# 3x3 convolution products as two 128x64 array tiles with two runs of 64 positions

## The chip, the cores and the metric

The kernel runs on one core of a Trainium2 chip. The metric is the device time of one execution in microseconds, as the median of several runs. A TensorE product of two float32 operands shows in the profile as two passes, each with one weight load (LDWEIGHTS, on the row called PEld) and one matrix multiplication (MATMUL, on the row called PE). In this text a *pass* is one such pair of records.

## What is computed

The input x has 8 images of 512 channels and 32x32 positions. After a group normalisation the layer computes, in float32:

```python
t = cbs(x, cv1_w, cv1_bn, 0)            # 1x1 convolution, batch norm, SiLU
ys = [t[:, :C], t[:, C:]]               # C = 256 channels each
for i in range(N):                      # N = 2
    yi = ys[-1]
    z = cbs(yi, m_cv1_w[i], m_cv1_bn[i], 1)              # the 3x3 convolution, 256 -> 256
    z = bot_attention(z, m_qkv_w[i], m_rw[i], m_rh[i])   # 4 heads of 64 over 1024 positions
    z = silu(bn_eval(conv2d(z, m_cv2_w[i], 0), m_cv2_bn[i]))
    ys.append(yi + z)
return cbs(concatenate(ys, axis=1), cv2_w, cv2_bn, 0)    # and x is added
```

The change concerns the line with the 3x3 convolution. It runs twice for each image, 16 times in all.

## The kernel before, in words

**Images and stages.** A Python loop runs over the 8 images, so the program is a straight list of instructions. For each image and each of the two bottlenecks the stages follow each other: `tiles_in` (VectorE transforms the input of the 3x3 convolution), `conv3x3`, the projection to queries, keys and values (`project_strassen`, lines L630 and L634, in image 0 a plain one), attention in a fast form (`attention_fast`), `m2` (L994). Between them lie the first 1x1 convolution of the next image (L386 or L1140) and the last one of this image (L1028). A scheduler orders the instructions of each engine when the program is built, by priorities and by the `issue_after` marks in the source; each engine then runs its own list in that order, with semaphores between engines.

**The 3x3 convolution.** It is done by a Winograd scheme: input and weights are transformed so that the convolution becomes sums of plain products, and the results are transformed back. `tiles_in` writes three tiles `vs[i]` (i = 0, 1, 2, called `v_in` in the profile), each with 2 channel blocks `k`, 2 rows, 4 columns and 128 positions. The weights `us[i]` have the same three pairs, made by `make_u` in image 0 (`u_new`) and loaded from DRAM afterwards (`u`), with 128 output channels for each block. For each half `oc` of the 256 output channels and each pair i, `conv3x3` takes a PSUM tile of 128 partitions x 2 rows x 4 columns x 128 positions[...]. It fills each of the eight blocks with a sum of two products over k (L970). A product has the whole 128x128 weight block as the stationary operand and 128 positions as the moving one. `columns_out` then reads the PSUM tile (ScalarE at L452, VectorE at L453 to L456), and `rows_out` (L473 to L481) finishes the transform.

**Other products that matter here.** In attention, the logits (L734) and the products with v (L768) use 64x64 tiles of the array, four of them side by side, over 512 positions. The row sums of attention (L786) use four tiles of 128 rows by 32 columns over 256 positions. All products of L386, L630, L634, L994, L1028 and L1140 use the whole 128x128 array.

**Order.** All products are in one queue of TensorE. SyncE issues loads, GpSimd issues stores and some loads; VectorE and ScalarE transform, evict PSUM and compute the exponentials. [...]

Of the kernel before, what the change touches and what calls it, by code (L numbers as in the profile page):

```python
# [56 lines left out]
HD = 64  # L57
# [4 lines left out]
def kernel(  # L62
# [16 lines left out]
    nc = tc.nc  # L79
# [5 lines left out]
    NM = C // P  # L85
# [233 lines left out]
    SLOT = (0, 1, 3, 2)  # L319
# [44 lines left out]
    def stages(act, small, ps_big, ps_av, n_pt):  # L364


        def silu(dst, src, k):

            return nc.scalar.activation(dst, src, AF.Silu, scale=sh[:, k : k + 1], bias=bh[:, k : k + 1])  # L369
# [3 lines left out]
        def table_of(func):  # L373

            return nc.scalar.activation(spare, zero, func)
# [73 lines left out]
        def columns_out(r, ps):  # L449

            m2 = act.tile([P, 2, NT * NW], F32, tag="h", name="m2", bufs=2)
            nc.scalar.copy(m2, ps[:, :, 2, :])  # L452
            nc.vector.tensor_tensor(r[..., 0], ps[:, :, 1, :], m2, ALU.add)  # L453
            nc.vector.tensor_tensor(r[..., 1], ps[:, :, 1, :], m2, ALU.subtract)
            nc.vector.scalar_tensor_tensor(r[..., 0], ps[:, :, 0, :], 2.0, r[..., 0], ALU.mult, ALU.add)
            nc.vector.scalar_tensor_tensor(r[..., 1], ps[:, :, 3, :], -2.0, r[..., 1], ALU.mult, ALU.add)  # L456

        def rows_out(dst, r12, r34, ends):


            sd = act.tile([P, 2, 2, NT * F], F32, tag="acc", name="sd", bufs=2)
            s_, d_, big_s, big_d = sd[:, 0, 0], sd[:, 0, 1], sd[:, 1, 0], sd[:, 1, 1]
            stt, tt = nc.vector.scalar_tensor_tensor, nc.vector.tensor_tensor

            def tiles(ap):
                return ap.rearrange("p (t w) -> p t w", w=F)

            def to(r):
                return dst.rearrange("p (t r w) -> p r t w", r=4, w=F)[:, r]

            def first():
                for i, rr in enumerate((r12, r34)):
                    tt(sd[:, i, 0], rr[:, 0], rr[:, 1], ALU.add)  # L473
                    tt(sd[:, i, 1], rr[:, 0], rr[:, 1], ALU.subtract)
                stt(to(1), tiles(big_d), -0.5, tiles(d_), ALU.mult, ALU.add)
                return tt(to(2), tiles(s_), tiles(big_s), ALU.subtract)

            def last():
                stt(ends, ends, -6.0, sd[:, 0], ALU.mult, ALU.add)
                stt(to(0), tiles(big_s), -0.25, tiles(ends[:, 0]), ALU.mult, ALU.add)  # L480
                stt(to(3), tiles(big_d), -2.0, tiles(ends[:, 1]), ALU.mult, ALU.add)  # L481

            return first, last
# [121 lines left out]
        def first_sum(z):  # L605

            t = act.tile([P, 4, HALF], F32, tag="pt", name="t_z", bufs=n_pt)
            nc.vector.tensor_tensor(t[:, 0], z[:, 0, ts(1, HALF)], z[:, 0, ts(0, HALF)], ALU.subtract)
            return t
# [345 lines left out]
        def conv3x3(n, vs, u_of, summed=False):  # L955
            t = None
            z = act.tile([P, NM, HW], F32, tag="z", name="z")
            for oc in range(NM):
                us = u_of(oc)
                r = act.tile([P, 2, 2, NT * NW, 2], F32, tag="acc", name="r_mid", bufs=2)  # L960
                ends = act.tile([P, 2, NT * NW, 2], F32, tag="rs", name="r_ends", bufs=2)
                rs = (r[:, 0], r[:, 1], ends)
                flat = [a.rearrange("p r q o -> p r (q o)") for a in rs]
                first, last = rows_out(z[:, oc, :], *flat)
                for i in range(PAIRS):
                    ps = ps_big.tile([P, 2, NC, NT * NW], F32, tag="big", name="c3_ps")
                    for row in range(2):
                        for col in range(NC):
                            for k in range(NM):
                                nc.tensor.matmul(  # L970
                                    ps[:, row, col, :], us[i][:, k, row, SLOT[col], :], vs[i][:, k, row, col, :],
                                    start=(k == 0), stop=(k == NM - 1),
                                )
                    columns_out(rs[i], ps)
                    if i == 1:
                        mid = first()
                        if oc == NM - 1 and summed:
                            with tc.issue_after(mid.ins):
                                t = first_sum(z)
                last()  # L980
                for half in range(NH):
                    part = z[:, oc, ts(half, HALF)]
                    last_silu = silu(part, part, bn_m1[n] + oc)
            with tc.issue_after(last_silu.ins):
                table_of(AF.Exp)
            return z, t
# [270 lines left out]
    us = {}  # L1257
# [63 lines left out]
    with tc.issue_after(made.ins):  # L1321
        vs = s.tiles_in(ypad[0])
    load_bottleneck(0)
    nxt = None
    for b in range(B):
# [6 lines left out]
        def u_of(n):  # L1332
            def of(oc):
                nonlocal last_load
                if b == 0 and n == 0 and oc == 1:
                    with tc.issue_after(last.ins):
                        for i in range(PAIRS):
                            make(n, oc, [i])
                got = [us.pop((oc, i)) if (oc, i) in us else load_u(n, oc, i) for i in range(PAIRS)]
                if (b > 0 or n > 0) and oc == 1:  # L1340
                    sq[n], last_load = load_sq(n)
                return got

            return of
# [40 lines left out]
        def first():  # L1385
            nonlocal nxt, six
            if more:
                nxt = new_y0()
            if more and b > 0:
                six = s.strassen_cv1(w1, sw, xs, nxt, y1n)  # L1390
                six[0]()
            elif more:
                s.cv1(w1, xs, nxt, y1n, Y1S[: NM // 2])
            else:
                parts[1] = s.cv2_part(w1, (y0, y1), 1)
# [34 lines left out]
        vs = s.tiles_in(y2)  # L1430
# [56 lines left out]
        if more:  # L1487
            three[2](y2, ylast, last, stored)
            with tc.issue_after(last.ins):
                vs = s.tiles_in(y1n)  # L1490
# [97 lines left out]
```

## Time and profile before

| | before |
|---|---|
| time, median of 3 runs | 2313.61 us (2312.37 to 2314.16) |
| span of the profiled execution, first to last instruction | 2311.5 us |
| the median run less this span | 2.1 us |
| TensorE multiplications, busy | 2286.2 us (99%) |
| TensorE weight loads, busy | 1172.4 us (51%) |
| VectorE, busy | 1840.2 us (80%) |
| ScalarE, busy | 987.6 us (43%) |
| granted TensorE clock, mean | 0.998 |
| products of the 3x3 convolutions (L970), busy | 306.1 us for 2720 passes and 41.5 us for 352 |

The profile comes from one execution. Its time is known as the span from the first to the last instruction; the device time of a run holds a little more around it. A busy time counts every moment in which an engine has at least one instruction under way, so overlapping matmuls are counted once, while the mean duration of one is longer than the distance from one to the next. A line number such as L970 is the line of the statement in the kernel's source.

### The profile page before, as it was taken

What the parts mean: (1) busy time and instruction counts of PE and PEld (TensorE: products, weight loads), DVE (VectorE), ACT (ScalarE), POOL (GpSimd) and SP (SyncE); (2) the same over time, 40 slices, a digit from 0 to 9 for tenths busy, and PEclk for the clock granted to TensorE, in tenths of its full rate; (3) what the DMA queues carried; (4) which work ended last, traced back from release to release, by engine and by line L of the source; (5) the groups of instructions that cost most, each with busy time, mean ns of one, the idle gap of its engine ahead of it and who ended that gap; (6) DMA issues with size and microseconds to landing.
All of it is one profiled execution on the core that took longest, in us unless ns stands there. A gap on an engine that the chain in (4) does not pass through costs nothing.

```text
span 2311.5 us, 36527 instructions
## 1 busy us (share of the span) xinstructions
PE 2286.2 (99%) x14806; PEld 1172.4 (51%) x14806; DVE 1840.2 (80%) x2920; ACT 987.6 (43%) x1292; POOL 89.1 (4%) x308
## 2 busy tenths in 40 slices
PE   7999999999999999999999999999999999999998
PEld 4546355463554636446364553646436364473643
DVE  8888878888788877887788887788877988777774
ACT  2443524435154452544525354253542525335352
POOL 1000000000000000000000000000000000000000
PEclk9999999999999999999999999999999999999999
DMA  7422333041430415213161221603116030260201
GB/s 239 174 86 87 120 134 154 16 151 34 174 118 26 136 48 202 76 53 108 52 240 37 76 87 47 250 29 102 59 47 250 29 133 29 75 221 16 87 11 62
DMA packets 95521, 235.60 MB, mean 102 GB/s; under 512 B 28016, under 2 KB 50736, under 8 KB 81904
## 3 DMA queue, kind: packets, MB, share of 16 engines
q1 hardware_dynamic: 83600, 182.84, 23.3%
q0 software_dynamic: 11744, 50.34, 5.7%
q8 instruction: 119, 1.95, 0.3%
q14 instruction: 58, 0.48, 0.1%
HBM read 198.54 MB, written 34.60 MB: 101 GB/s over the span
## 4 chain that ended last, share of the span: by engine, by line
PE 96%; DVE 3%; ACT 0%; DMA 0%; POOL 0%; issue 0%; SPq 0%; DVEq 0%; ACTq 0%
PE av_ps L768 19%; PE l_ps L734 19%; PE c_ps L970 14%; PE c L1028 8%; PE p_ps L630 8%; PE x_ps L1140 6%; PE c_new L1028 6%; PE m_ps L994 5%; PE ps L386 4%; PE pv_ps L634 3%; PE s_ps L786 1%; PE p_ps L634 1%; PE s_ps L804 1%; DVE acc L754 0%; PE v_ps L595 0%; DMA x<-in_x_dram 0%
## 5 line engine op out<-in xcount | busy, mean ns | idle before, releaser
L738 ACT ACTIVATE pt<-l_ps 128x1024 f32<-128x1024 f32 x512 | 494.8, 1023 | 410.1 <-PE l_ps L734 385.5
L754 DVE TENSOR_TENSOR acc<-acc,pt 128x1024 f32<-128x1024 f32 x384 | 469.5, 1223 | 65.5 <-ACT pt L738 40.0
L768 PE MATMUL av_ps<-pt,vT 64*64 64x512 f32 x4096 | 486.4, 591 | 0.5 <-DVE ao L776 0.5
L734 PE MATMUL l_ps<-q,kr 64*64 64x512 f32 x4096 | 485.9, 590 | 0.0
L970 PEld LDWEIGHTS c_ps<-v_in,u 128*128 128x128 f32 x2720 | 306.0, 192 | 6.7 <-issue 6.7
L970 PE MATMUL c_ps<-v_in,u 128*128 128x128 f32 x2720 | 306.1, 275 | 0.0
L768 PEld LDWEIGHTS av_ps<-pt,vT 64*64 64x64 f32 x4096 | 159.2, 133 | 269.4 <-issue 225.1
L734 PEld LDWEIGHTS l_ps<-q,kr 64*64 64x64 f32 x4096 | 160.0, 133 | 263.3 <-issue 252.2
L452 ACT COPY m<-c_ps 128x256 f32<-128x256 f32 x96 | 35.4, 369 | 216.3 <-PE c_ps L970 213.6
L1028 PE MATMUL c_new<-t_in,ws 128*128 128x512 f32 x288 | 124.6, 592 | 0.0
L994 PE MATMUL m_ps<-ao,m_sb 128*128 128x512 f32 x256 | 112.5, 592 | 0.0
L369 ACT ACTIVATE m_kept<-m_kept,bh,sh 128x512 f32<-128x512 f32 x42 | 31.9, 805 | 146.0 <-DVE m_kept L1112 86.3
L752 DVE TENSOR_TENSOR acc<-pt 128x1024 f32<-128x1024 f32 x64 | 78.1, 1220 | 18.0 <-ACT pt L738 18.0
L1028 PEld LDWEIGHTS c_new<-t_in,ws 128*128 128x128 f32 x288 | 54.7, 190 | 68.9 <-issue 66.0
L630 PE MATMUL p_ps<-t_z,sq 128*128 128x512 f32 x180 | 87.1, 593 | 0.0
L369 ACT ACTIVATE t<-m_ps,bh,sh 128x512 f32<-128x512 f32 x64 | 48.1, 776 | 83.9 <-PE m_ps L994 82.5
L994 PEld LDWEIGHTS m_ps<-ao,m_sb 128*128 128x128 f32 x256 | 48.6, 190 | 61.2 <-issue 61.0
L369 ACT ACTIVATE z<-z,bh,sh 128x512 f32<-128x512 f32 x64 | 48.6, 806 | 56.1 <-DVE z L481 56.1
L1002 DVE TENSOR_TENSOR ylast<-t,ypad 128x512 f32<-128x512 f32 x32 | 22.0, 692 | 63.2 <-ACT t L369 63.2
L445 DVE TENSOR_TENSOR v_in<-w_rows 128x512 f32<-128x512 f32 x96 | 65.6, 683 | 0.0
L453 DVE TENSOR_TENSOR r_mid<-c_ps,m 128x256 f32<-128x256 f32 x64 | 27.1, 423 | 46.5 <-ACT m L452 46.5
L1028 PE MATMUL c<-ypad,ws 128*128 128x512 f32 x144 | 63.8, 592 | 0.0
(255 smaller groups left out, 2997.3 us busy)
## 6 DMA issues: line engine op xcount, KB each, us to landing
u<-u SPq DMA_DIRECT2D x85, 1024.0 KB
x<-in_x_dram SPq DMA_DIRECT2D x32, 512.0 KB
x_res<-in_x_dram POOLq DMA_DIRECT2D x32, 512.0 KB, 6.9
out_dram<-m_kept POOLq DMA_DIRECT2D x28, 512.0 KB, 7.3
u<-u_new POOLq DMA_DIRECT2D x12, 1024.0 KB, 6.3
w<-in_cv_w_dram SPq DMA_DIRECT2D x12, 1024.0 KB
rs<-r_dram SPq DMA_DIRECT2D x96, 128.0 KB
ws<-s SPq DMA_DIRECT2D x24, 512.0 KB
```

The costliest lines, as they stand in the source:

```text
L369: return nc.scalar.activation(dst, src, AF.Silu, scale=sh[:, k : k + 1], bias=bh[:, k : k + 1])
L386: last_product[0] = nc.tensor.matmul(ps[:, half, :], w_of(k), rhs_of(k, half), start=(k == begin), stop=(k == end))
L630: nc.tensor.matmul(ps[:, o, :], w[:, o, :], rhs, start=not onto, stop=True, skip_group_check=onto)
L634: nc.tensor.matmul(v[:, ts(j, P)], rhs[:, ts(j, P)], w[:, 2, :], start=j == 0 and not onto, stop=True, skip_group_check=True,)
L734: nc.tensor.matmul(ps[kh * HD : (kh + 1) * HD, hd, :], kr[r, c, o : o + HD], q[r, c, ts(half, HALF)], start=True, stop=True,)
L738: exp = nc.scalar.activation(pt[:, i], ps, AF.Exp, scale=SCALE)
L754: ins = nc.vector.tensor_tensor(accs[g], accs[g], pt[:, i], ALU.add)
L768: nc.tensor.matmul(avs[g][hd * HD : (hd + 1) * HD, kh, :], vT[r, j, o : o + HD], pt[r, i, hd, :], start=(j == 0), stop=(j == NJ - 1),)
L970: nc.tensor.matmul(ps[:, row, col, :], us[i][:, k, row, SLOT[col], :], vs[i][:, k, row, col, :], start=(k == 0), stop=(k == NM - 1),)
L994: nc.tensor.matmul(pss[oc][:, half, :], m2_sb[:, n, k, ts(oc, P)], ao[:, k, ts(half, HALF)], start=(k == 0), stop=(k == NM - 1),)
L1028: nc.tensor.matmul(ps[:, o, :], w[:, k, ts(o, P)], rhs[part][:, c, :], start=(k == 0 and not onto), stop=(k == KB - 1), skip_group_check=onto,
L1140: nc.tensor.matmul(ps[:, o, :], w[:, c, ts(o, P)], rhs[c], start=(c == 0 and not onto), stop=(c == 1), skip_group_check=onto,)
```

## The change

Each product of L970 is written as four smaller ones. The 128 output channels are split in two halves `h`, which go to partitions 0 to 63 and 64 to 127 of the same PSUM block; each half has a weight block of 128 rows by 64 columns, so that the two halves are two tiles of the array side by side. The 128 positions are split in two runs `part` of 64 neighbouring ones. The order is: first run with both halves, second run with both halves. Each half loads its weights again for the second run. Within a block only the first run of the first k carries the start flag[...].

```diff
                     for row in range(2):
                         for col in range(NC):
                             for k in range(NM):
-                                nc.tensor.matmul(
-                                    ps[:, row, col, :], us[i][:, k, row, SLOT[col], :], vs[i][:, k, row, col, :],
-                                    start=(k == 0), stop=(k == NM - 1),
-                                )
+                                for part in range(2):
+                                    w = slice(part * HD, (part + 1) * HD)
+                                    for h in range(2):
+                                        o = slice(h * HD, (h + 1) * HD)
+                                        nc.tensor.matmul(
+                                            ps[o, row, col, w], us[i][:, k, row, SLOT[col], o],
+                                            vs[i][:, k, row, col, w],
+                                            start=(k == 0 and part == 0), stop=(k == NM - 1 and part == 1),
+                                            skip_group_check=True,
+                                        )
                     columns_out(rs[i], ps)
```

HD is 64, NM is 2, NC is 4. Nothing else in the source differs.

## The prediction

> **What bounds the kernel now.** I began with the busy times of the page and the chain that ended last.
>
> ```profile
> PE 2286.2 (99%) x14806; PEld 1172.4 (51%) x14806; DVE 1840.2 (80%) x2920; ACT 987.6 (43%) x1292; POOL 89.1 (4%) x308
> PE 96%; DVE 3%; ACT 0%; DMA 0%; POOL 0%; issue 0%; SPq 0%; DVEq 0%; ACTq 0%
> ```
>
> The first line gives busy time, share of the span and instruction count for each engine; the second gives the shares of the chain. TensorE has work 99% of the time and is 96% of the chain. What lengthens the TensorE stream lengthens the kernel, and no other engine can hide it.
>
> Next I read the groups of instructions. The changed statement is L970:
>
> ```profile
> L970 PEld LDWEIGHTS c_ps<-v_in,u 128*128 128x128 f32 x2720 | 306.0, 192 | 6.7 <-issue 6.7
> L970 PE MATMUL c_ps<-v_in,u 128*128 128x128 f32 x2720 | 306.1, 275 | 0.0
> L970 PE MATMUL c_ps<-v_in,u_new 128*128 128x128 f32 x352 | 41.5, 281 | 3.2 <-DVE u_new L344 3.2
> ```
>
> Busy time comes after the bar, then the mean ns of one, then the idle time before. 2720+352 = 3072 records are two float32 passes of each of 1536 products (8 images x 2 convolutions x 2 output halves x 3 pairs x 2 rows x 4 columns x 2 k). They cost 306.1+41.5 = 347.6 us, 15% of the span. In this line alone the weight loads are busy as long as the products: a load lies under every product and is as long as it. The idle 3.2 us of the last line is one wait in image 0.
>
> The timeline gives the pace, which a mean duration does not, since matmuls overlap (columns: start, length, engine, line, count):
>
> ```profile
> 184.82 18.03 PE L970 MATMUL c_ps<-v_in,u_new 128*128 128x128 f32 x160
> 206.25 1.88 PE L630 MATMUL p_ps<-z,qkv_sb 128*128 128x512 f32 x4
> ...
> 107.43 1.04 PE L734 MATMUL l_ps<-q,kr 64*64 64x512 f32 x8
> 108.39 0.64 PE L786 MATMUL s_ps<-acc,ones 128*32 128x256 f32 x8
> ```
>
> 160 passes in 18.03 us: (18.03-0.275)/159 = 111.7 ns from one to the next with 128 positions. Four in 1.88: (1.88-0.593)/3 = 429 ns with 512. A straight line through both is 0.826 ns a position plus 5.9 ns a pass. The last two lines show tiles: eight 64x64 passes are two rounds of four, 0.43 us apart, and eight 128x32 passes of 256 positions take 0.64 us, where one after another they would need 8 x 0.21 = 1.7.
>
> Last, the loads of tiles:
>
> ```profile
> 108.39 0.16 PEld L786 LDWEIGHTS s_ps<-acc,ones 128*32 128x32 f32 x8 [0.81 <-issue]
> 109.52 0.21 PEld L768 LDWEIGHTS av_ps<-pt,vT 64*64 64x64 f32 x8 [0.97 <-DVE ao L776]
> 110.01 0.15 PEld L768 LDWEIGHTS av_ps<-pt,vT 64*64 64x64 f32 x4 [0.28 <-issue]
> ```
>
> Eight loads of 128 rows by 32 columns take 0.16 us where one takes 0.108: loads into different column tiles run at once, with all 128 rows. Four 64-column loads take 0.15 and eight 0.21, so a tile's second load follows its first by some 0.06 us.
>
> [...] loads of 128, 64 and 32 columns last 192, 133 and 108 ns. [...] the round before L786 starts at 107.86 (107.43+0.43), so the next begins 0.53 after it instead of 0.43. A change of mode costs 0.10. [...]
>
> **The change part by part.**
> - *Products.* One pass of 128 columns by 128 positions becomes two rounds; in a round two 64-column tiles run side by side over 64 positions. By the line, a round is 64 x 0.826 + 5.9 = 58.8 ns, two are 117.6. The positions cost the same; what is added is a second hand-over, 5.9 ns. Over 3072 passes: +18.1 us.
> - *Loads.* Four 64-column loads stand where one of 128 was (the second run reloads the same weights). Each tile loads 64 columns per 64 positions, the same ratio as now, so load and product stay equally long. Loads of the two tiles overlap as at L786, so no term beyond the hand-over. [...]
> - *Modes.* The convolution's neighbours (L1028, L1140 or L386 before, L630 after) are 128x128, and its own mode is now 128x64. Two changes in each of 16 convolutions: 32 x 0.10 = +3.2 us.
> - *Instructions.* 3072 loads and as many matmuls become 12288 of each: 18432 more, and four to issue in 58.8 ns, one per 14.7 ns. The page's instruction queue moved 1.95 MB for 29612 TensorE instructions, 66 bytes each, in 119 packets. A packet (about 250 instructions) took 0.3% x 16 x 2311.5/119 = 0.9 us, and 250 instructions will last 3.7 us, so fetching should stay hidden. Issuing is the open term; I take none and give it to a rival.
> - *Other engines.* The built program keeps the order of TensorE, SyncE and GpSimd otherwise. VectorE and ScalarE change order only around image 0's weight transforms; the first of the second output half come earlier, which could save the 3.2 us wait. VectorE is packed there, so I expect the next weights to be late instead: -3 to +2, taken as 0. Elsewhere VectorE and ScalarE wait for c_ps; they wait longer, at no cost. PSUM tiles and semaphore groups stay.
>
> Sum: 18.1 + 3.2 = 21.3 us. Against the profiled span of 2311.5 this is 2332.8; the median of the runs, 2313.6, is 2.1 above that span, which gives 2335.
>
> **The rivals.**
> - *The front of TensorE becomes the bound.* It decides above 14.7 ns an instruction. For it: nothing in this trace issues steadily faster than two per 111.7 ns. Against it: after the first wait, at 8.07 us, four loads and four matmuls have all ended by 8.48, so short bursts are quick; but those may come from a queue. [...]
> - *The tiles do not overlap with 128 rows each.* Then four turns of 58.8 = 235 per old pass: +379, with the modes 2696. The lines of L786 speak against it.
> - *Not slower: a tile's hand-over is shorter.* [...] It decides below 56 ns a round. Against it: the gap is wide where load and product are equally long, and they stay so.
>
> **How the numbers follow.** Main case 65%, front-end bound 20%[...], tiles in turn 5%, short hand-over 10%. About 0.2%, 4.6 us, can be told from no change. Faster than that needs the short hand-over and the saved wait in image 0: 4%. Within it: the rest of that rival and the low edge of the main case, 10%. Slower: 86%. The range runs from 2308 (short hand-over with the wait saved) to 2395[...]; left out are [...] the tiles in turn, and a little below. The main case's own range is 2312 to 2355.
>
> **What would show it.** Right: L970's successor has 12288 matmul records, a busy total near 366 us, and 29 or 30 ns between neighbouring starts; the load group stays equally busy; each convolution starts and ends with 0.1 us more gap. Issue bound: the pace is a fixed number above 58.8 a round. Tiles in turn: no two tiles' starts closer than their length, and a stage of twice the time. [...] I am wrong if time appears outside the convolutions, in waits of TensorE for VectorE or ScalarE.

## The result, and the profile after

The changed kernel takes 2414.26 us (median; 2413.48 to 2415.31), the kernel before 2313.6 on the same chip: a ratio of 1.0436, 95% interval 1.0423 to 1.0448. It is 101 us slower, where I had forecast 21. The profiled execution has a span of 2412.6 us.

The page of the changed kernel, busy times and chain:

```profile
PE 2327.6 (96%) x24022; PEld 1202.0 (50%) x24022; DVE 1840.5 (76%) x2920; ACT 988.3 (41%) x1292; POOL 89.1 (4%) x308
PE 94%; DVE 3%; issue 3%; ACT 0%; POOL 0%; DMA 0%; DVEq 0%; ACTq 0%
```

TensorE still carries the chain, but a new entry stands beside it: "issue", 3% of the span, time in which TensorE waited for nothing that the profile shows. Before, it was 0%. VectorE and ScalarE do what they did. The groups of the changed statement, now L974, say where it is:

```profile
L974 PE MATMUL c_ps<-v_in,u 128*64 128x64 f32 x10880 | 340.2, 226 | 55.8 <-issue 55.5
L974 PEld LDWEIGHTS c_ps<-v_in,u 128*64 128x64 f32 x10880 | 332.5, 141 | 72.1 <-issue 66.7
L974 PE MATMUL c_ps<-v_in,u_new 128*64 128x64 f32 x1408 | 43.7, 226 | 5.1 <-DVE u_new L340 3.1 <-issue 1.9
```

The two groups of attention have the same busy times as before to the tenth, and the only other TensorE group that moved by more than half a microsecond is the one that follows a convolution (L630 `p_ps<-z,qkv_sb`, from 56.5 to 58.0 us). The "issue" idle time of the matmuls is all in the convolutions. The wait of image 0 for VectorE (3.1 us) stayed, as assumed. The timeline of the first convolution of image 1, first in the kernel before, then in the changed one, shows what the idle time is made of (start, length, engine, line, count, idle before):

```profile
338.24 21.60 PE L970 MATMUL c_ps<-v_in,u 128*128 128x128 f32 x192
359.68 1.88 PE L630 MATMUL p_ps<-z,qkv_sb 128*128 128x512 f32 x4
```

```profile
343.05 6.22 PE L974 MATMUL c_ps<-v_in,u 128*64 128x64 f32 x205
351.74 3.95 PE L974 MATMUL c_ps<-v_in,u 128*64 128x64 f32 x127 [2.46 <-issue]
356.01 3.95 PE L974 MATMUL c_ps<-v_in,u 128*64 128x64 f32 x128 [0.32 <-issue]
362.76 3.94 PE L974 MATMUL c_ps<-v_in,u 128*64 128x64 f32 x127 [2.80 <-issue]
368.40 5.52 PE L974 MATMUL c_ps<-v_in,u 128*64 128x64 f32 x181 [1.70 <-issue]
373.85 1.55 PE L630 MATMUL p_ps<-z,qkv_sb 128*128 128x512 f32 x3
```

The count is the figure to look at: TensorE stops, runs 127 or 128 matmuls, and stops again. 128 matmuls and their 128 loads are 256 instructions. That is also what a packet on the instruction queue holds:

```profile
q8 instruction: 191, 3.13, 0.5%
```

(packets, MB, share of the DMA engines; before: 119 packets, 1.95 MB). There are 72 packets more for 18432 instructions more, which is 256 for each; and a packet has 16 KB (1.18 MB in these 72), so an instruction has 64 bytes. Between the stops nothing is wrong: 128 matmuls in 3.95 us are 64 rounds at (3.95-0.222)/63 = 59 ns, the forecast pace being 58.8.

The trace also has the DMA packets one by one. Set beside the starts of the matmuls, those of the instruction queue in this convolution read:

| TensorE starts a block | next instruction packet starts | ends | TensorE goes on after its stop |
|---|---|---|---|
| 351.73 | 353.80 | 354.73 | 356.01 |
| 356.01 | 360.40 | 361.42 | 362.75 |
| 362.75 | 365.99 | 367.09 | 368.40 |
| 368.40 | 369.67 | 370.65 | no stop |

So one block is fetched while the one before it runs. In these four blocks a fetch takes 1.3 us at the least until its packet starts, 0.9 to 1.1 us for the packet, and another 1.3 us or a little more until TensorE goes on: about 3.5 us together. A block of the changed kernel runs 3.76 us (64 rounds of 58.8 ns). When the packet starts later, TensorE stops.

In what follows a stop, or gap, is a distance of more than 0.2 us from one matmul's start to the next one's. (The idle time of the profile counts from the end of the earlier matmul, some 0.2 us later, so it comes to less: 55.5 and 1.9 us.) Of the 46 gaps inside the convolutions the first is the wait for VectorE; the other 45 all end 1.2 to 1.6 us after the end of an instruction packet. They also stand where blocks begin: in a count by 256 through all of TensorE's instructions (loads, matmuls and semaphore waits), the first matmul after each of the 45 has the same place, give or take one. The same holds, within two places, for every gap outside image 0's first convolution in the versions below that have any.

### The profile page after: what moved, and what is told of

The parts are those of the page before. It is cut to its first block, busy times and chain, and to the rows that moved or that the text cites. A ratio compares the mean times of both kernels' runs of the same rounds, so it can differ in the third digit from the quotient of the medians.

```text
span 2412.6 us, 54959 instructions
## 1 busy us (share of the span) xinstructions
PE 2327.6 (96%) x24022; PEld 1202.0 (50%) x24022; DVE 1840.5 (76%) x2920; ACT 988.3 (41%) x1292; POOL 89.1 (4%) x308
## 4 chain that ended last, share of the span: by engine, by line
PE 94%; DVE 3%; issue 3%; ACT 0%; POOL 0%; DMA 0%; DVEq 0%; ACTq 0%
PE av_ps L768 18%; PE l_ps L734 18%; PE c_ps L974 15%; PE c L1034 8%; PE p_ps L630 8%; PE x_ps L1146 6%; PE c_new L1034 6%; PE m_ps L1000 5%; PE ps L386 4%; PE pv_ps L634 3%; PE s_ps L786 1%; PE p_ps L634 1%; PE s_ps L804 1%; DVE acc L754 0%; PE v_ps L595 0%
## 5 line engine op out<-in xcount | busy, mean ns | idle before, releaser
L974 PE MATMUL c_ps<-v_in,u 128*64 128x64 f32 x10880 | 340.2, 226 | 55.8 <-issue 55.5
L974 PEld LDWEIGHTS c_ps<-v_in,u 128*64 128x64 f32 x10880 | 332.5, 141 | 72.1 <-issue 66.7
L752 DVE TENSOR_TENSOR acc<-pt 128x1024 f32<-128x1024 f32 x64 | 78.0, 1219 | 18.1 <-ACT pt L738 18.1
L630 PE MATMUL p_ps<-t_z,sq 128*128 128x512 f32 x180 | 87.1, 593 | 0.0
```

The source lines that it names most:

```text
L630: nc.tensor.matmul(ps[:, o, :], w[:, o, :], rhs, start=not onto, stop=True, skip_group_check=onto)
L974: nc.tensor.matmul(ps[o, row, col, w], us[i][:, k, row, SLOT[col], o], vs[i][:, k, row, col, w], start=(k == 0 and part == 0), stop=(k == ...
```

## The experiments

Each is shown as an edit of the changed kernel's loop. *More traffic* adds copies, and the last one also changes the projection; the others change nothing else. The excerpts leave out the start and stop flags, which follow the loops, and in both versions with quarters the argument `tile_position=(0, h * 32)`. My theory after the result: **instruction fetch**, as just described. The rivals are named with each.

**Only the halves.** One run of 128 positions:

```diff
-for part in range(2):
-    w = slice(part * HD, (part + 1) * HD)
-    for h in range(2):
-        ... ps[o, row, col, w], us[i][:, k, row, SLOT[col], o], vs[i][:, k, row, col, w] ...
+for h in range(2):
+    ... ps[o, row, col, :], us[i][:, k, row, SLOT[col], o], vs[i][:, k, row, col, :] ...
```

> Only the split of the channels: two 128x64 tiles side by side, each over all 128 positions, so half the instructions of the change. Theory (instruction fetch): TensorE's instructions come in blocks of 256, the next block is asked for when the present one starts, and a stall is what the fetch lasts beyond the block. Here 256 instructions last 7.1 us, against 3.6 to 7.1 us that a fetch took in the changed kernel: 0 to 3 us of stalls in all. With two changes of mode per convolution (+3 us) that makes 2317 us if each pass keeps a hand-over of 5.9 ns[...]. Rival (tiles of 128 rows stall TensorE by themselves): the stalls stay, half or all of them, 2340 to 2390 us.

Measured: 2311.05 us, against 2313.47 before; ratio 0.999, interval 0.9983 to 0.9996. It is a little faster than the kernel before, by 2.4 us, and the fastest version here; it is 6 us below the 2317 of the forecast, which kept 5.9 ns between passes. The timeline of the same convolution, from its predecessor to its successor:

```profile
338.34 0.59 PE L1030 MATMUL c_new<-t_in,w 128*128 128x512 f32 x1
338.86 21.18 PE L972 MATMUL c_ps<-v_in,u 128*64 128x128 f32 x384
359.97 1.99 PE L630 MATMUL p_ps<-z,qkv_sb 128*128 128x512 f32 x4
```

384 matmuls without a stop, and (21.18-0.273)/191 = 109.4 ns a round instead of 111.7. So two tiles of 128 rows run side by side without any loss, and with a load shorter than its product the hand-over is smaller. The first line shows the price of the mode on the way in: the next group starts 0.52 us after a matmul that otherwise gives way after 0.43. The way back is dearer. L630 starts 0.20 us after the last matmul's start (359.97 against 360.04-0.27), where a round of 0.11 would have let it start, and its four matmuls take 1.99 us instead of the 1.88 of the kernel before: some 0.20 us in all. Both ways together, 0.29 us in 16 convolutions, cost 4.7 us; the shorter rounds save about 7; that leaves about 2.3, and 2.4 were measured. The rival, that such tiles stall by themselves, is refuted.

**Only the runs.** The whole array, two runs:

```diff
 for part in range(2):
     w = slice(part * HD, (part + 1) * HD)
-    for h in range(2):
-        ... ps[o, row, col, w], us[i][:, k, row, SLOT[col], o], vs[i][:, k, row, col, w] ...
+    ... ps[:, row, col, w], us[i][:, k, row, SLOT[col], :], vs[i][:, k, row, col, w] ...
```

> Only the split of the positions: the whole 128x128 array, two runs of 64, half the instructions of the change. Theory (the load sets the pace when it is longer than the product): each run must load 128 columns[...] 2628 to 2657 us, and no stall of a block, since 256 instructions last 14 us. Rival (only a second hand-over of 5.9 ns, loads of the same weights hidden or skipped): 2332 us.

Measured: 2651.46 us, ratio 1.1458 (1.1441 to 1.1476), inside the forecast; the rival's 2332 is out.

```profile
376.57 42.99 PE L972 MATMUL c_ps<-v_in,u 128*128 128x64 f32 x384
```

(42.99-0.22)/383 = 111.7 ns for a run of 64 positions, exactly what a run of 128 took: the load of 128 columns sets the pace, and loading the same weights again is not skipped. There is no stop; 256 instructions last 14 us here. In the change, where each tile loads half the columns, two runs took 2 x 59 ns and not 2 x 111.7.

**One run in every second row.**

```diff
-for part in range(2):
-    w = slice(part * HD, (part + 1) * HD)
+parts = 2 if row == 0 else 1
+for part in range(parts):
+    w = slice(part * P // parts, (part + 1) * P // parts)
     ...
```

> Row 0 as in the change (two tiles, two runs of 64), row 1 with two tiles and one run of 128. Theory (instruction fetch): 256 instructions last 4.9 us on average instead of 3.76, so each stall of the changed kernel is 1.13 us shorter: 26 us of 68 are left, in 25 stalls instead of 46, and all start at a multiple of 256 instructions; hand-over 9 us, modes 3, half clock after stalls up to 3: 2350 to 2358 us. Rival (a cost of each run of 64 positions): exactly half of the change's excess, 2364 us, with as many stalls in row 0 as before.

Measured: 2354.27 us (ratio 1.0175, 1.0159 to 1.019), inside the forecast of the fetch theory and 10 us below that of the rival. Outside image 0's first convolution there are 28 us in 25 gaps; 26 in 25 were forecast, and all 25 stand where a block of 256 begins. The blocks are now longer and the stops shorter (a line of the timeline merges what follows each other, under the shape of its first matmul):

```profile
349.20 4.77 PE L975 MATMUL c_ps<-v_in,u 128*64 128x64 f32 x128 [0.20 <-issue]
355.06 5.07 PE L975 MATMUL c_ps<-v_in,u 128*64 128x64 f32 x127 [1.09 <-issue]
361.18 4.97 PE L975 MATMUL c_ps<-v_in,u 128*64 128x128 f32 x117 [1.05 <-issue]
```

Again 127 or 128 matmuls between two stops (the last line runs to the end of the convolution), though the rows, and with them the kinds of run, change elsewhere.

**Quarters.** Four tiles of 32 columns, one run of 128 positions:

```diff
-for part in range(2): ...
-    for h in range(2):
-        o = slice(h * HD, (h + 1) * HD)
+for h in range(4):
+    o = slice(h * 32, (h + 1) * 32)
     ...
```

> Four 128x32 tiles side by side, each over all 128 positions: as many instructions as the change, at the same rate, but no second run and no second hand-over. Theory (instruction fetch): the stalls stay, 65 us or so with 10 us of half clock after them, modes 3 us[...]: 2375 to 2395 us. Rival (the runs of 64 positions stall, or the reloading of the same weights): no stalls, 2306 to 2318 us.

Measured: 2404.18 us (1.0394, 1.0372 to 1.0416; single runs 2397.75 to 2411.61). The stops are there without a single run of 64, which refutes the rival:

```profile
354.06 3.70 PE L972 MATMUL c_ps<-v_in,u 128*32 128x128 f32 x127 [2.57 <-issue]
358.32 3.70 PE L972 MATMUL c_ps<-v_in,u 128*32 128x128 f32 x128 [0.57 <-issue]
```

It is 9 us above my range. A block lasts 3.70 us here from first start to last end, of which the last matmul's own length is 0.27, so about 3.5 from block to block instead of 3.76; by this estimate 0.26 us more of stop in each of some 46 stopping blocks would be 12 us. The trace has 10 more: 78 us in 54 gaps outside image 0's first convolution, where the change has 68 in 45. My forecast left out that the fetch takes a faster pace back.

**Quarters and runs.** Four tiles of 32 columns and two runs, twice the instructions of the change:

```diff
 for part in range(2):
     w = slice(part * HD, (part + 1) * HD)
-    for h in range(2):
-        o = slice(h * HD, (h + 1) * HD)
+    for h in range(4):
+        o = slice(h * 32, (h + 1) * 32)
         ...
```

> Four 128x32 tiles and two runs of 64: twice the instructions of the change, one per 7.4 ns. Theory (instruction fetch): 256 instructions last 1.9 us, less than any fetch, so every one of 192 blocks lasts as long as a fetch, 3.6 us at the least and some 4.3 on average: 826 us for the convolutions instead of 347, about 2790 us (2650 to 2900). Rival (stalls belong to tiles or runs, as many for each as in the change): 2420 to 2500 us.

Measured: 2764.85 us (1.1947, 1.1929 to 1.1966). The fetch is now the pace of the whole convolution:

```profile
391.82 6.34 PE L974 MATMUL c_ps<-v_in,u 128*32 128x64 f32 x255 [5.53 <-issue]
400.03 1.99 PE L974 MATMUL c_ps<-v_in,u 128*32 128x64 f32 x128 [1.87 <-issue]
403.92 1.99 PE L974 MATMUL c_ps<-v_in,u 128*32 128x64 f32 x128 [1.89 <-issue]
410.39 1.93 PE L974 MATMUL c_ps<-v_in,u 128*32 128x64 f32 x79 [4.48 <-issue]
```

In the two middle lines 128 matmuls run in 2 us, then TensorE waits about as long. (In the first line most of the time passes at half the clock, the mean granted clock of the run being 0.958; two blocks take 6.3 us and no stop falls between them; the last is cut off by the end of the view.) The 16 convolutions take 789 us for 192 blocks: 4.1 us a block, where the theory said 4.3 (826 us); the rival's total would have left some 450 to 530 us for them. From one stop to the next it is 3.3 us at the least, so that is the shortest fetch of all the runs, and up to 7.0. Within a block one instruction follows the other in (1.99-0.22)/256 = 7 ns, so no slower pace of single instructions lies behind the stops.

**More traffic.** The question here is why a fetch is sometimes some 3.5 us and sometimes 7:

```diff
+if oc == 0 and n == 1 and summed:
+    for _ in range(4):
+        nc.gpsimd.dma_start(<a new DRAM tile>, z[:, 0, :])
```

> The changed kernel, with four extra copies of 512 KB from SBUF to DRAM issued from GpSimd in each second convolution of an image, once its first output half is done; nobody reads them. Theory (the fetch waits behind data in the DMA engines): the stalls of the second convolutions, 21 us in eight, grow by 1 to 3 us each, 10 to 20 us in all; the first convolutions, 50 us, stay: 2424 to 2436 us. Rival (the wait of the fetch has nothing to do with the data traffic): 2414 us, within 4.

Measured: 2436.95 us (1.0533, 1.0517 to 1.0549), 23 us more than the change, 1 us above the range and far outside the rival's. The gaps in the second convolutions, where the copies are, went from 21.0 to 38.9 us; in the first convolutions of images 1 to 7 from 46.7 to 47.2. An example is the second convolution of image 3, in the changed kernel and then with the copies:

```profile
1076.52 18.38 PE L974 MATMUL c_ps<-v_in,u 128*64 128x64 f32 x617
1095.61 4.78 PE L974 MATMUL c_ps<-v_in,u 128*64 128x64 f32 x151 [0.70 <-issue]
```

```profile
1087.98 18.33 PE L974 MATMUL c_ps<-v_in,u 128*64 128x64 f32 x617
1107.29 3.95 PE L974 MATMUL c_ps<-v_in,u 128*64 128x64 f32 x127 [0.98 <-issue]
1114.16 0.92 PE L974 MATMUL c_ps<-v_in,u 128*64 128x64 f32 x24 [2.93 <-issue]
```

Up to the copies both run alike; after them one stop grows and a new one of 2.9 us appears. So the fetch of instructions waits longer when there is more data to move. The table above says the same: while the packets waited for 2.1, 4.4 and 3.2 us the DMA engines were 75, 85 and 97% busy, and 39% for the one that waited 1.3. It also fits the pattern of the change itself: the first convolution of an image, in which x, u and the stores of the last image are moved (302 to 320 GB/s in four of them), stops for 6.7 us on average, the second (226 to 265 GB/s in four) for 2.6.

**Halves in the projection too.** The first experiment, with L630 and L634 in 128x64 tiles as well:

```diff
-nc.tensor.matmul(ps[:, o, :], w[:, o, :], rhs, ...)
+for h in range(2):
+    r = slice(h * HD, (h + 1) * HD)
+    nc.tensor.matmul(ps[r, o, :], w[:, o, r], rhs, ...)
...
-nc.tensor.matmul(v[:, ts(j, P)], rhs[:, ts(j, P)], w[:, 2, :], ...)
+for h in range(2):
+    r = slice(h * HD, (h + 1) * HD)
+    nc.tensor.matmul(v[r, ts(j, P)], rhs[:, j * P + h * HD : j * P + (h + 1) * HD], w[:, 2, :], ...)
```

> The halves of the first experiment, and the products of project_strassen (L630 and L634) in 128x64 tiles too, so that convolution and projection share a mode. Theory: 840 passes of L634 lose 2.2 ns each as the convolution's did (-1.8 us), L630 with 512 positions stays, and 15 changes of mode between them go (-1.4 us): 2308 us. Rival (the gain of the halves is of another kind, and more tile instructions cost): 2311 us or more.

Measured: 2324.85 us (1.0047, 1.0033 to 1.0061). The forecast was wrong. The convolutions are as fast as with the halves alone (before image 1's second projection 140 matmuls in 7.81 us, 109.2 ns a round), and the 0.20 us after them are gone (L632 starts 0.10 us after the last matmul's start and takes 1.89 us), but each projection is longer: after image 1's second convolution it runs from 491.44 to 510.94 us, 19.5 us, where it took 489.30 to 507.74, 18.4 us, before; 15 times 1.05 us is 16, and less the 5 us that the convolutions gain it makes the loss of 11. Part of it is a wait of 0.20 us for ScalarE (L666) in each projection, 2.9 us in all, which the kernel before does not have. For the rest, the trace has products of two lines in turn:

```profile
503.93 0.59 PE L632 MATMUL p_ps<-t_z,sq 128*64 128x512 f32 x1
504.03 0.49 PE L638 MATMUL p_ps<-sq,t_z 128*64 128x128 f32 x3
504.36 0.59 PE L632 MATMUL p_ps<-t_z,sq 128*64 128x512 f32 x1
```

This reads as one tile at long products (L632) while the other is already at the short ones (L638), though the trace does not name the tile. That the tiles fall out of step, and that this is the cause of the loss, was not tested.

## Why the prediction was wrong

The direction was right, and the parts that I had priced came within 2 us; a part that I had priced at nothing, with what follows from it, was three quarters of the result. The spans differ by 101.1 us. What the trace of the changed kernel gives for each:

| part | forecast | measured |
|---|---|---|
| second hand-over: pace of a round 58.8 ns | +18.1 | 59 ns, about +19 |
| changes of mode, 32 | +3.2 | 0.09 us in, 0.20 out, +4.7 |
| fetching of instructions: stops in convolutions 2 to 16 | 0 | +65 (45 stops) |
| one stop at the end of a convolution | 0 | +2.7 |
| half clock after stops | 0 | about +9 |
| image 0, waits for VectorE or ScalarE | 0 | within 1 |

The parts come to about 100 us. The time of a stop is taken here less the 59 ns of a round. The one at the end of a convolution stands before L630, at 669.97 us in image 2; the profile puts it down to VectorE (L479), but the weight load starts at 669.94, before that VectorE instruction is done, and 1.5 us after the end of an instruction packet, at the place where a block begins. So it is a stop of the same kind.

- *Products, loads, modes.* Products and loads were right within a microsecond. A change of mode was read only on the way into a narrower mode; the way back costs 0.20 us and not 0.10, so the modes cost 4.7 us where 3.2 were forecast. The straight line through the paces of 128 and 512 positions gave 58.8 ns for 64. The reading of L786, that loads and products of 128-row tiles overlap, was right too: tiles in turn are out. The halves add a correction: the 5.9 ns of the line is not one constant. With a load of 64 columns under 128 positions the pace fell to 109.4 ns; with 128 columns under 128 positions it is 111.7, and with 64 under 64 it is 59. So the change keeps the wide gap and pays it twice. The rival of the short hand-over, and with it the low end of my range, rested on an estimate of the gap that no trace had shown. The kernel before gives a figure: its 28 passes of 256 positions from 78.06 us on (L595) are (6.21-0.379)/27 = 216 ns apart, where passes of 512 positions are 429 apart. That is 0.83 ns a position, which leaves some 3 ns at 256 and 512 positions and some 5 at 128. One reading was too narrow, without effect here: loads as busy as their products are not in L970 alone, but in L634 too (31.5 and 31.6 us for each of two groups).
- *Instructions: the step that failed.* I wrote that a packet takes 0.9 us, that 250 instructions last 3.7 us, "so fetching should stay hidden". 0.9 us is the time of the packet alone. The fetch also has some 1.3 us before it and 1.3 us after it, and more before it when the DMA engines are busy; and only one block is under way at a time: with quarters and runs TensorE used a block up in 2 us and got one in 4.1, and after none of its 160 stops outside image 0's first convolution did the next packet start earlier than 1.0 us after TensorE had gone on. So the comparison was 3.7 us against 0.9, and should have been 3.76 against 3.5 to 7. The margin was next to nothing, in a stage where the kernel before already keeps the DMA engines 58% busy (183.9 to 205.4 us, against 36% in the attention after it). That fetching stays hidden was an estimate of mine and not shown; the version with quarters and runs has 7 ns an instruction within a block and the change 14.7, and in both TensorE stops for the next block.
- *The half clock.* Beyond one in image 0, which the kernel before has too, the clock records have six stretches of 3.4 us at half clock in convolutions (granted 0.50, the first from 944.8 to 948.2 us); each begins 2 to 4 us after the start of a stop of 2.2 to 3.3 us. They cost 1.3 to 1.6 us each. There are twelve such stops in the convolutions, so only every second one has such a stretch after it. The versions without stops, *only the halves* and *only the runs*, have no such stretch in a convolution (mean granted clock 0.999 in both, against 0.994 in the change). That the stops bring them is likely from this, but no run tests it alone.
- *The rival.* I had "the front of TensorE becomes the bound" with 20%, but as a fixed pace of single instructions, by an estimate that no trace had shown. The place was right and the mechanism was not: single instructions are quick (7 ns with quarters and runs), and the supply comes in blocks of 256. The end of the range, 2395, came from that estimate and was too low. What I named as its sign, a fixed number above 58.8 ns a round, did not appear; the sign was idle time marked "issue" every 128 matmuls.

## What to carry to other kernels

Splitting products multiplies instructions, and TensorE has to be fed with them: count the time that 256 instructions last, here 3.8 us, and compare it with the whole of a fetch (here 3.3 us at the least, up to 7 while the DMA engines are busy), not with its packet. At 7.0 us a block, with the halves alone, nothing was lost; at 4.9 us on average 28 us of stops were left; at 3.8 us the kernel lost 77 us. If a narrow tile is wanted, keep the runs long: the halves with 128 positions have a load that is shorter than its product, and were 0.1% faster than the whole array.

## What the runs showed of the hardware that I had not expected

- One instruction block of TensorE is 256 instructions, 16 KB, and one is fetched while the one before it runs: in the convolution shown 1.3 to 4.4 us until the packet starts and 0.9 to 1.1 us for it, and in all 45 stops 1.2 to 1.6 us from its end until TensorE goes on.
- With quarters and runs, 2 us of work in each block, this path gave one block in 4.1 us on average, about 4 GB/s.
- Going from 128x128 products to 128x64 tiles cost 0.09 us, going back 0.20.
- Extra copies of 2 MB in a convolution lengthened its stops by 2.2 us on average (17.9 us in eight).
- A 64-column load under a product of 128 positions leaves some 3 ns between products, a 128-column load some 5 (109.4 and 111.7 ns, against 106.5, which is 128 positions at the 0.832 ns by which passes of 256 and 512 positions differ).
